# A four-layer graph network: the last batch's last tiles taken bank by bank, its output stored in three parts, the due times of layers 1 to 3 replaced

## The chip, the cores and the metric

The kernel runs on one core of a Trainium2 chip. A core has TensorE (PE; PEld is its weight load), VectorE (DVE), ScalarE (ACT), GpSimd (POOL) and SyncE (SP, which here issues most of the DMAs). The metric is the device time of one execution in microseconds (us). PSUM, where PE writes, has eight banks here, tiles `psc0` to `psc7`, each 128 x 512 f32.

## What is computed

There are 16 batches of 1024 nodes with 128 features, and an adjacency matrix for each. Every layer is x + gnn(relu(layernorm(x))). Layer 0 is a graph convolution with batch norms over all batches, so layers 1 to 3 can start only when all of it is done. Layer 1 and 3 are attention layers, layer 2 is one with scores from dot products. Cut to what matters:

```python
# layer 1 and layer 3 (layer 3 with an elu around it)
Wh = h @ W
e = leaky_relu((Wh @ a1)[:, :, None] + (Wh @ a2)[:, None, :])
out = softmax(where(adj > 0, e, -inf)) @ Wh
# layer 2
e = einsum('bid,bjd,dk->bkij', hidden, hidden, A)      # by the type of the edge, then leaky_relu
out = softmax(where(adj == 1, e[:, 0], ...)) @ hidden
```

## The kernel before, in words

**Tiles.** A batch is eight tiles of 128 nodes. The attention weights of one product are eight tiles `q[m]` of 128 x 1024 f32; they lie in ten rooms of SBUF (`xg6` to `xg15` in the profile's names) which all batches share. The product (`product`, L946) multiplies them with the values `v` of 128 x 129 (128 features and a column that sums the weights). Its output for the eight tiles of nodes lies in three PSUM banks, with three, three and two tiles (`TRI`). The weights of tile m give one step, here called a part: 8 matmuls that the profile counts as 16, L955, the banks in turn. So all three banks are complete only with the eighth part.

**A batch in layers 1 to 3** is the function `batch`. Layer 1 (`gat`, L989): norm, transpose (L932), scores and values (L996), the exponentials; the row of u is spread over all partitions, for the first batches by matmuls (L1034), for the others by a transpose (L1016), a copy (L1019), a send to DRAM (L1022) and a fetch from there (L1025). Then DVE weighs eight tiles (L1060), PE does eight parts, and `finish` takes reciprocals (L967), scales on ACT (L973) and adds (L985). Layer 2: norm with the power on POOL (L915) and the centring on DVE (L925), score matmuls in chunks of up to 512 columns (L1091), for each chunk two exponentials on ACT (L1099, L1095), larger and mask on DVE (L1109, L1112), transposes of the symmetric half (L1123) and their mask (L1127), eight parts, `finish`. Layer 3: `gat` again, then for each bank the reciprocal (L1141), two scalings for each tile of nodes on ACT (L1147), a join of two instructions on DVE (L1151, L1153). When all three banks are joined, one DMA of 512 KB stores the batch (L1161).

**Order.** Nothing is issued in the order in which it stands. Each piece of work is a step with an engine, an assumed duration, what it reads and writes and what rooms it needs. `Plan.attempt` places the steps one after another: for each engine it takes, among the steps that could begin within `WITHIN` of the earliest, the one with the lowest rank, and the rank is the due time of the step's batch less the longest assumed path from the step to the end. The result is a fixed order of instructions on each engine and a fixed room for each tile, PSUM banks included; the chip runs each engine's list in order, with waits between the engines. `DUES` has one due time for each batch, by its place in `order`: first the three batches whose adjacency is still in SBUF (13, 14, 15), then 0 to 12. A place is called a slot: slot 0 is batch 13, slot 15 is batch 12. At the same time some four batches are under way in different layers.

```python
rank = [due(s.group) - s.tail for s in self.steps]
...
order = sorted(kept["at"]) + [b for b in range(B) if b not in kept["at"]]
for b in order:
    batch(b)
plan.emit(lambda b: DUES[order.index(b)], WITHIN)
```

Of the kernel before, what the change touches and what calls it, by code (L numbers as in the profile page):

```python
# [19 lines left out]
P = 128  # L20

PAIRED = "(w p t) d -> p w t d"
# [11 lines left out]
LEVEL = 1638.0  # L34
XG_TILES = 6
WEIGHTS_AT = 40.0
L0_DUES, L0_WITHIN = [
    3.2, 51.2, 72.4, 90.5, 112.6, 124.5, 191.4, 204.9, 159.2, 265.6, 223.0, 273.4, 306.2, 325.8, 419.8, 408.3,
    419.5, 419.5,
], 0.1  # L40
DUES, WITHIN = [
    44.9, 60.2, 111.5, 81.6, 101.9, 124.9, 146.4, 167.9, 189.8, 211.1, 232.7, 254.2, 275.8, 297.5, 314.3,
    312.2,
], 0.02
GAT_LIMIT = 30.0
DOT_KEEP = 60.0
# [17 lines left out]
class Plan:  # L64
# [11 lines left out]
    def room(self, kind):  # L76
        return Room(kind)
# [10 lines left out]
    def step(self, engine, us, run, reads=(), writes=(), moved=0, group=0, also=(), since=0.0):  # L88
        s = Step(engine, us, run, moved, group, since)
        for k in reads:  # L90
            if k in self.writer:
                s.after.add(self.writer[k])
        for k in writes:
            if k in self.writer:
                s.after.add(self.writer[k])
            s.after.update(self.readers.get(k, ()))
        for k in reads:
            self.readers.setdefault(k, []).append(s)
        for k in writes:
            self.writer[k] = s  # L100
            self.readers[k] = []
        s.after.discard(s)
        for k in (*reads, *writes, *also):
            room = k[0] if isinstance(k, tuple) else k
            if isinstance(room, Room) and room not in s.rooms:
                s.rooms.append(room)
                room.uses += 1
        self.steps.append(s)
        return s
# [100 lines left out]
def groups_of(n, k):  # L210
    return [range(a, min(a + k, n)) for a in range(0, n, k)]
# [3 lines left out]
def gnn_stack(ctx: ExitStack, tc: tile.TileContext, x, adj, k1, b1, g1, be1, k2, b2, g2, be2,  # L215
# [52 lines left out]
    with tc.If(any_type == 0) as both:  # L268
        with tc.manual_schedule():
            plain_layers(tc, q_tiles, x, out, adj_t, gt_rows, u_rows, ident, ident_h, mhalf, gat1, gat3, edge, shift,  # L270
                         kcs, q9, rows9, held, kept)
# [5 lines left out]
def load_weights(nc, plan, rooms, tc, k1, b1, g1, be1, k2, b2, g2, be2, w1, a1, e0, w3, a3, edge, CB):  # L277
# [7 lines left out]
    def fetch(t, *parts):  # L285
        for n, (dst, src) in enumerate(parts):
            plan.step("sp", 0.1, lambda dst=dst, src=src: nc.sync.dma_start(dst(t), src), (),
                      [(id(t), n) if n else id(t)], 4096, 2, since=WEIGHTS_AT)

# [263 lines left out]
def norms(nc, plan, w, qall, q9, rows9, ident, ones, mhalf, gat1, gat3, edge, shift, kcs, flag, count):  # L553
# [93 lines left out]

    plan.step("dve", 0.8, choose, (), ["masks"], 0, 4, since=WEIGHTS_AT)
    group[0] = B + 1
# [141 lines left out]
def plain_layers(tc, q_tiles, x, out, adj_t, gt_rows, u_rows, ident, ident_h, mhalf, gat1, gat3, edge, shift,  # L791
                 kcs, q9, rows9, held, kept):
    nc = tc.nc
    B, N, D = x.shape
    NB = N // P
    WX = D + 3
    V1 = D + 1
    TRI = groups_of(NB, 3)
    ROW = [sum(NB - k for k in range(m)) * P for m in range(NB)]

    with ExitStack() as ctx:
# [28 lines left out]
            nc.gpsimd.memset(t, 0.0)  # L830
        for t in kinds["h1"]:
            nc.gpsimd.memset(t[:, :, D:V1], 1.0)
        plan = Plan(kinds)
        room = plan.room

        def batch(b):
            seat = room("seat")

            def step(engine, us_, run, reads=(), writes=(), moved=0, also=()):
                plan.step(engine, us_, run, reads, writes, moved, b, (seat, *also))  # L840
# [10 lines left out]
            at = plan.settled("at", kept["at"][b]) if b in kept["at"] else room("at")  # L851
# [94 lines left out]
            def ahead(m, acc):  # L946
                return acc if m > 2 else []

            def product(weights, done, values, V, acc):

                for m in range(NB):
                    def part(m=m):
                        for g, ns in enumerate(TRI):
                            for k, n in enumerate(ns):
                                nc.tensor.matmul(acc[g].ap[:, k * V1 : (k + 1) * V1],  # L955
                                                 weights[m].ap[:, n * P : (n + 1) * P], values.ap[:, m, :],
                                                 start=(m == 0 and k == 0), stop=(m == NB - 1),
                                                 skip_group_check=True)

                    step("pe", 1.88, part, [*done[m], *V], acc)  # L960
                return acc

            def over_sums(acc):
# [25 lines left out]
            def gat(layer, ext):  # L989
                y, gt, rs = norm(False)  # L990
                sc, ex, er, v, ub = (room(k) for k in ("tri", "tri", "col", "v", "ub"))
# [64 lines left out]
                q = [room("q") for _ in range(NB)]  # L1056
                acc = [room("ps") for _ in TRI]
                for m in range(NB):
# [2 lines left out]
                                                       ALU.max, ALU.mult)  # L1061

                    step("dve", 1.2, weigh, [(ub, 0), (ub, 4), ex, at], [q[m]], also=ahead(m, acc))
                return product(q, [[k] for k in q], v, [(v, "e"), *((v, ns[0]) for ns in TRI)], acc)

            finish(gat(1, gat1))

            y, ht, _ = norm(True)
# [10 lines left out]
            q = [room("q") for _ in range(NB)]  # L1079
            acc = [room("ps") for _ in TRI]  # L1080
            eu = room("eu")
            done = []
            for m in range(NB):
                e = room("e")
                wide = (NB - m) * P
                chunks = [range(c, min(c + 512, wide)) for c in range(0, wide, 512)]
                for c in chunks:
# [14 lines left out]
                    part = len(c) / 512  # L1102
# [28 lines left out]
                step("dve", 0.1 + 1.12 * wide / N, mask, [(eu, m), at], [(q[m], "u")], also=ahead(m, acc))  # L1131
                done.append([(q[m], "u"), *((q[m], ks[0]) for ks in groups_of(m, 4))])
            finish(product(q, done, h1, [h1], acc))

            acc = gat(3, gat3)
            rc, e3, r3 = room("col"), room("y"), room("y")
            for g, ns in enumerate(TRI):
# [19 lines left out]
                step("act", 0.52 * len(ns), scale, [acc[g], (rc, g)], [(e3, g), (r3, g)])  # L1157
                step("dve", 0.12 + 0.28 * len(ns), join, [(e3, g), (r3, g), *(X[n] for n in ns)], [(e3, g)])

            def store():  # L1160
                nc.sync.dma_start(out[b].rearrange(PAIRED, p=P, t=2), e3.ap.rearrange("p (w t) d -> p w t d", t=2))  # L1161

            step("sp", 0.06, store, [(e3, g) for g in range(3)], [("out", b)], P * N * 4)

        order = sorted(kept["at"]) + [b for b in range(B) if b not in kept["at"]]
        for b in order:
            batch(b)
        plan.emit(lambda b: DUES[order.index(b)], WITHIN)
# [493 lines left out]
```

## Time and profile before

| what | us |
|---|---|
| median of 3 runs (lowest, highest) | 1447.16 (1446.58, 1447.86) |
| the profiled execution | 1446.24 |
| its span in the profile | 1444.4 |
| PE busy, layers 1 to 3 well under way (600 to 800) | 197.34 of 200 |
| PE waiting, 420 to 1300, by the list of waits | ACT exponentials L1095 2.1 before L1091, masks L1127 2.0 before L1123 and 1.7 before L955 |
| granted clock 0.50 | from 368.1 to 378.3, between layer 0 and layer 1 |
| last matmul ends | 1433.1 |
| last join on DVE ends | 1438.5 |
| 512 KB stores, issue to landing | 2.9 to 3.8, median 3.0 |

How to read it: an engine's row in a timeline is start, duration, engine, line, operation, out<-in and the count of instructions in it; in square brackets stands the idle time just before, with the one who ended it. The list of stretches gives, for each engine, the time it was busy in a stretch. Matmuls overlap in their pipeline, so a busy PE can hide small waits; the distance between starts tells more, and that of L955's matmuls is 0.112 us.

### The profile page before, as it was taken

What the parts mean: (1) busy time and instruction counts of PE and PEld (TensorE: products, weight loads), DVE (VectorE), ACT (ScalarE), POOL (GpSimd) and SP (SyncE); (2) the same over time, 40 slices, a digit from 0 to 9 for tenths busy, and PEclk for the clock granted to TensorE, in tenths of its full rate; (3) what the DMA queues carried; (4) which work ended last, traced back from release to release, by engine and by line L of the source; (5) the groups of instructions that cost most, each with busy time, mean ns of one, the idle gap of its engine ahead of it and who ended that gap; (6) DMA issues with size and microseconds to landing.
All of it is one profiled execution on the core that took longest, in us unless ns stands there. A gap on an engine that the chain in (4) does not pass through costs nothing.

```text
span 1444.4 us, 30384 instructions
## 1 busy us (share of the span) xinstructions
PE 1389.4 (96%) x11710; PEld 1269.4 (88%) x11710; DVE 1105.2 (77%) x3154; ACT 794.6 (55%) x2123; POOL 366.1 (25%) x472
## 2 busy tenths in 40 slices
PE   4999999999999999999999999999999999999996
PEld 3889999898888999998989999898998898798896
DVE  4877665545778798897978878888889787797676
ACT  3766776765544763656464554636464744634652
POOL 7787677553310110110110101101111002010010
PEclk9999999999899999999999999999999999999998
DMA  9988988860300012111111212111111101010101
GB/s 157 150 179 163 142 144 148 140 66 2 117 1 16 31 45 88 60 45 59 45 60 45 74 39 91 61 47 60 45 59 45 45 30 45 16 44 16 45 31 47
DMA packets 56348, 99.05 MB, mean 69 GB/s; under 512 B 6297, under 2 KB 45569, under 8 KB 52865
## 3 DMA queue, kind: packets, MB, share of 16 engines
q1 hardware_dynamic: 37472, 79.17, 15.5%
q0 software_dynamic: 18720, 17.83, 14.3%
q8 instruction: 94, 1.54, 0.4%
q14 instruction: 62, 0.50, 0.1%
HBM read 118.37 MB, written 28.95 MB: 102 GB/s over the span
## 4 chain that ended last, share of the span: by engine, by line
PE 68%; DVE 18%; ACT 7%; DMA 3%; POOL 2%; issue 1%; DVEq 0%; POOLq 0%; ACTq 0%; SPq 0%
PE psc L955 31%; PE psa L498 7%; PE psa L458 7%; DVE xg L1060 6%; PE psc L1091 6%; PE gram L351 4%; PE psc L996 3%; PE psc L885 2%; PE psc L932 2%; DVE st L903 2%; ACT y L928 2%; PE psa L417 2%; PE psc L1123 2%; ACT eu L1099 2%; DVE y L925 2%; ACT e L1095 2%
## 5 line engine op out<-in xcount | busy, mean ns | idle before, releaser
L955 PE MATMUL psc<-v,xg 128*128 128x129 f32 x4096 | 483.1, 276 | 1.7 <-DVE xg L1060 1.3
L955 PEld LDWEIGHTS psc<-v,xg 128*128 128x128 f32 x4096 | 472.2, 192 | 14.2 <-issue 7.2
L955 PEld LDWEIGHTS psc<-h,xg 128*128 128x128 f32 x2048 | 239.4, 192 | 14.7 <-DVE xg L1127 6.5
L955 PE MATMUL psc<-h,xg 128*128 128x129 f32 x2048 | 249.7, 277 | 2.2 <-DVE xg L1127 1.7
L914 POOL TENSOR_SCALAR col<-mv 128x8 f32<-128x8 f32 x48 | 22.8, 475 | 896.1 <-DVE mv L909 722.0
L1060 DVE SCALAR_TENSOR_TENSOR xg<-ub,tri,at 128x1024 f32<-128x1024 f32 x176 | 217.5, 1276 | 9.4 <-DMA at<-adj_t 4.7
L1099 ACT ACTIVATE eu<-psc,shift 128x512 f32<-128x512 f32 x192 | 114.4, 596 | 162.8 <-PE psc L1091 150.1
L1091 PE MATMUL psc<-gt,gt 128*128 128x512 f32 (+3 forms) x384 | 152.7, 497 | 7.1 <-ACT e L1095 3.6
L425 ACT ACTIVATE at<-psa 128x1024 fp8e4<-128x1024 fp8e4 x128 | 131.3, 1033 | 42.1 <-PE psa L417 38.3
L1109 DVE SCALAR_TENSOR_TENSOR eu<-e,shift,eu 128x1024 f32<-128x1024 f32 (+7 forms) x128 | 103.8, 812 | 44.2 <-ACT e L1095 43.4
L458 PE MATMUL psa<-hv,a 128*128 128x257 f16 x1024 | 119.7, 276 | 4.3 <-DVE hv L400 3.3
L498 PE MATMUL psa<-rv,at 128*128 128x259 f16 x1024 | 119.6, 275 | 2.2 <-DVE g L505 2.0
L458 PEld LDWEIGHTS <-a 128*128 128x128 fp8e4 x1024 | 100.8, 99 | 19.6 <-issue 4.6
L498 PEld LDWEIGHTS <-at 128*128 128x128 fp8e4 x1024 | 99.6, 98 | 18.2 <-issue 2.7
L1095 ACT ACTIVATE e<-psc,shift 128x512 f32<-128x512 f32 x192 | 114.1, 594 | 0.0
L928 ACT ACTIVATE y<-xg,col 128x128 f32<-128x128 f32 x256 | 78.4, 394 | 56.9 <-DVE col L911 56.9
L973 ACT ACTIVATE y<-psc,col 128x128 f32<-128x128 f32 x256 | 71.2, 394 | 67.1 <-DVE col L967 47.7
L1147 ACT ACTIVATE y<-psc,col 128x128 f32<-128x128 f32 x256 | 69.1, 407 | 58.3 <-DVE col L1141 58.3
L1060 DVE SCALAR_TENSOR_TENSOR xg<-ub,tri,atc 128x1024 f32<-128x1024 f32 x80 | 98.9, 1276 | 0.8 <-DMA atc<-adj_t 0.8
L915 POOL TENSOR_TENSOR col<-col,mhalf 128x8 f32<-128x8 f32 x48 | 96.9, 2018 | 4.0
L470 POOL TENSOR_SCALAR rv<-r,cola 128x128 f16<-128x128 f32 x128 | 82.1, 651 | 59.5 <-DVE r L466 59.1
L1091 PEld LDWEIGHTS psc<-gt,gt 128*128 128x128 f32 x384 | 60.6, 191 | 32.0 <-issue 14.6
(214 smaller groups left out, 2004.0 us busy)
## 6 DMA issues: line engine op xcount, KB each, us to landing
a<-in_adj_dram POOLq DMA_DIRECT2D x128, 128.0 KB, 7.9
ub<-u_rows SPq DMA_DIRECT2D x29, 512.0 KB
xb<-in_x_dram SPq DMA_DIRECT2D x27, 512.0 KB, 5.6
adj_t<-at SPq DMA_DIRECT2D x13, 1024.0 KB, 4.3
at<-adj_t SPq DMA_DIRECT2D x8, 1024.0 KB, 4.8
out_dram<-y SPq DMA_DIRECT2D x16, 512.0 KB, 3.0
gt_rows<-xg SPq DMA_DIRECT2D x13, 512.0 KB, 8.4
xg<-gt_rows SPq DMA_DIRECT2D x13, 512.0 KB
```

The lines of the kernel that those rows point to most:

```text
L425: nc.scalar.activation(at.ap[:, i, :], ps.ap.bitcast(F8)[:, t::2], AF.Square, saturate=False, accum_out=sums.ap[:, i : i + 1])
L458: nc.tensor.matmul(ps.ap[:, : 2 * D + 1], block[:, i % 2 :: 2], hv.ap[:, j, :], start=(j == 0), stop=(j == NB - 1))
L470: nc.gpsimd.tensor_scalar_mul(rv.ap[:, i, 0:D], r.ap[:, i, :D], rc.ap[:, i : i + 1])
L498: nc.tensor.matmul(ps.ap[:, :W2], at.ap[:, i, j * P : (j + 1) * P], rv.ap[:, i, :], start=(i == 0), stop=(i == NB - 1))
L915: nc.gpsimd.tensor_tensor(rs.ap, va.ap, mhalf, ALU.pow)
L928: nc.scalar.activation(y.ap[:, n, :], xs(n), AF.Relu, bias=nm.ap[:, n : n + 1])
L955: nc.tensor.matmul(acc[g].ap[:, k * V1 : (k + 1) * V1], weights[m].ap[:, n * P : (n + 1) * P], values.ap[:, m, :], start=(m == 0 and k == ...
L1060: nc.vector.scalar_tensor_tensor(q[m].ap, ub.ap, ex.ap[:, m, 1:2], at.ap[:, m, :], ALU.max, ALU.mult)
L1091: nc.tensor.matmul(ps.ap[:, : len(c)], ha.ap[:, m * P : (m + 1) * P], ht.ap[:, m * P + c[0] : m * P + c[-1] + 1], start=True, stop=True)
L1095: nc.scalar.activation(e.ap[:, c[0] : c[-1] + 1], ps.ap[:, : len(c)], AF.Exp, bias=shift[:, 0:1], scale=1.0 - SLOPE)
L1099: nc.scalar.activation(eu.ap[:, ROW[m] + c[0] : ROW[m] + c[-1] + 1], ps.ap[:, : len(c)], AF.Exp, bias=shift[:, 1:2], scale=SLOPE)
L1109: nc.vector.scalar_tensor_tensor(t, e.ap[:, :wide], shift[:, 2:3], t, ALU.max, ALU.mult)
```

## The change

Three things. In layer 3 of the last batch in `order` (slot 15) the product does its first four tiles of weights as before; the last four become three steps, one for each bank, each with the four tiles' matmuls into that bank. The store of that batch becomes three DMAs: the first pair of node tiles (128 KB) when bank 0 is joined, two pairs (256 KB) when bank 1 is, the last pair (128 KB) when bank 2 is. And the sixteen due times are others, which gives all batches in layers 1 to 3 another order; layer 0 keeps its own.

```diff
+WHOLE = 4
 DUES, WITHIN = [
-    44.9, 60.2, 111.5, 81.6, 101.9, 124.9, 146.4, 167.9, 189.8, 211.1, 232.7, 254.2, 275.8, 297.5, 314.3,
-    312.2,
+    26.3, 47.2, 238.9, 112.2, 133.2, 154.3, 175.7, 197.2, 218.8, 240.4, 261.9, 283.6, 305.2, 326.7, 341.4,
+    341.6,
 ], 0.02
...
-            def product(weights, done, values, V, acc):
+            def product(weights, done, values, V, acc, whole=NB):
...
+                def part(ms, gs):
+                    for g in gs:
+                        for m in ms:
+                            for k, n in enumerate(TRI[g]):
                                 nc.tensor.matmul(acc[g].ap[:, k * V1 : (k + 1) * V1],
                                                  weights[m].ap[:, n * P : (n + 1) * P], values.ap[:, m, :],
                                                  start=(m == 0 and k == 0), stop=(m == NB - 1),
                                                  skip_group_check=True)
...
+                for m in range(whole):
+                    step("pe", 1.88, lambda m=m: part([m], range(len(TRI))), [*done[m], *V], acc)
+                left = range(whole, NB)
+                if left:
+                    for g, ns in enumerate(TRI):
+                        step("pe", 0.235 * len(ns) * len(left), lambda g=g: part(left, [g]),
+                             [*(d for m in left for d in done[m]), *V], [acc[g]])
...
-                return product(q, [[k] for k in q], v, [(v, "e"), *((v, ns[0]) for ns in TRI)], acc)
+                return product(q, [[k] for k in q], v, [(v, "e"), *((v, ns[0]) for ns in TRI)], acc,
+                               WHOLE if layer == 3 and b == order[-1] else NB)
...
+            if b != order[-1]:
+                step("sp", 0.06, lambda: store(slice(0, NB // 2)), [(e3, g) for g in range(len(TRI))], [("out", b)], P * N * 4)
+            else:
+                pairs = [min((ns[-1] + 1) // 2, NB // 2) for ns in TRI]
+                for g, n in enumerate(pairs):
+                    some = slice(pairs[g - 1] if g else 0, n)
+                    step("sp", 0.06, lambda some=some: store(some), [(e3, k) for k in range(g + 1)], [("out", b, g)], P * N * 4 * (some.stop - some.start) // (NB // 2))
```

By the instruction lists of the two built programs the lists of layer 0 are equal; from layer 1 on each engine's list has the same pieces of work in another order, except for the three bank steps and the two added stores. Slot 2's part of the work keeps its place late in the list (behind slot 12's), slots 14 and 15 change their parts in it: in the program before, slot 14 is the last to end, after the change slot 15.

More of the change, by code (lines that the diff above doesn't have):

```diff
@@ L832, in plain_layers @@
             nc.gpsimd.memset(t[:, :, D:V1], 1.0)
+        order = sorted(kept["at"]) + [b for b in range(B) if b not in kept["at"]]
         plan = Plan(kinds)
@@ L947, in ahead @@
                 return acc if m > 2 else []
-            def product(weights, done, values, V, acc):
[L951 to L954, printed above, removed]
+            def product(weights, done, values, V, acc, whole=NB):
[3 more added lines that the diff above has]
+                            for k, n in enumerate(TRI[g]):
                                 nc.tensor.matmul(acc[g].ap[:, k * V1 : (k + 1) * V1],
@@ L958, in part @@
                                                  skip_group_check=True)
-                    step("pe", 1.88, part, [*done[m], *V], acc)
+                for m in range(whole):
[5 more added lines that the diff above has]
+                             [*(d for m in left for d in done[m]), *V], [acc[g]])
                 return acc
@@ L1158, in batch, with store @@
                 step("dve", 0.12 + 0.28 * len(ns), join, [(e3, g), (r3, g), *(X[n] for n in ns)], [(e3, g)])
[L1160 to L1165, printed above, removed]
+            def store(some):
+                nc.sync.dma_start(out[b].rearrange(PAIRED, p=P, t=2)[:, some],
+                                  e3.ap.rearrange("p (w t) d -> p w t d", t=2)[:, some])
+            if b != order[-1]:
[5 more added lines that the diff above has]
+                    step("sp", 0.06, lambda some=some: store(some), [(e3, k) for k in range(g + 1)], [("out", b, g)], P * N * 4 * (some.stop - some.start) // (NB // 2))
         for b in order:
```

## The prediction

> **What bounds the kernel now.** I read the page's busy line first, then the stretches around the change, then the last 45 us engine by engine. A batch is called by its place in `order`: slot 0 to slot 15. Slot 15 is batch 12, the one the diff treats apart; slot 14 is batch 11. A "part" is the 16 L955 matmuls that use one tile of weights. The busy line, then stretches of the trace:
>
> ```profile
> PE 1389.4 (96%) x11710; PEld 1269.4 (88%) x11710; DVE 1105.2 (77%) x3154; ACT 794.6 (55%) x2123; POOL 366.1 (25%) x472
> ...
> ```
> ```profile
> 405.00:440.00 35.00, 32.64 (x254) 29.05 (x253) 24.24 (x58) 20.13 (x54) 5.31 (x3) 1.00 0.00 0
> 1389.00:1433.00 44.00, 43.79 (x391) 43.44 (x390) 30.96 (x64) 17.76 (x63) 3.00 (x2) 1.00 0.11 38
> 1433.00:1439.00 6.00, 0.08 (x1) 0.00 (x0) 4.06 (x12) 4.30 (x16) 0.00 (x0) 0.79 0.28 94
> 1439.00:1445.00 6.00, 0.00 (x0) 0.00 (x0) 0.00 (x0) 0.00 (x0) 0.00 (x0) 0.50 0.27 93
> ```
> The columns are PE, PEld, DVE, ACT and POOL busy, then the granted clock. PE is full until 1433 (43.79 of 44), and after it nothing is left but ACT, DVE and a store. So the time is PE's work, plus the holes in PE, plus the drain behind its last matmul. The change leaves PE's work alone: the same matmuls, each still loading its own weights. Only holes and drain can move.
>
> **The drain before.** DVE, ACT, then the SP queue:
> ```profile
> 1429.54 0.17 DVE L1141 RECIPROCAL col<-psc 128x2 f32<-128x2 f32 x1 [0.27 <-PE psc L955]
> ...
> 1433.94 0.16 DVE L1141 RECIPROCAL col<-psc 128x2 f32<-128x2 f32 x1
> 1435.03 0.56 DVE L1151 SCALAR_TENSOR_TENSOR y<-y,y 128x384 f32<-128x384 f32 x1 [0.93 <-ACT y L1147]
> ...
> 1437.64 0.42 DVE L1151 SCALAR_TENSOR_TENSOR y<-y,y 128x256 f32<-128x256 f32 x1
> 1438.10 0.42 DVE L1153 SCALAR_TENSOR_TENSOR y<-y,xg 128x256 f32<-128x256 f32 x1
> ```
> ```profile
> 1428.70 4.23 ACT L1147 ACTIVATE y<-psc,col 128x128 f32<-128x128 f32 x16 [19.67 <-DVE col L1141]
> 1433.27 4.30 ACT L1147 ACTIVATE y<-psc,col 128x128 f32<-128x128 f32 x16 [0.34 <-DVE col L1141]
> ```
> ```profile
> 1400.79 0.29 SPq L1022 DMA_DIRECT2D u_rows<-ur  x1
> 1402.02 0.32 SPq L1025 DMA_DIRECT2D ub<-u_rows  x1
> 1410.18 28.78 SPq L1161 DMA_DIRECT2D out_dram<-y  x3
> ```
> The last two batches end together, so ACT scales one (16 instructions, 0.265 apart) and then the other; DVE takes the reciprocals of their third banks at 1429.54 and 1433.94. PE's end is 1433.08 (T); the last join ends 1438.52 (T+5.4); the last store is issued 1438.6, lands about 3.0 later (median of the 512 KB stores), and the program ends at 1444.4 (T+11.3).
>
> **The drain after.** In the built program's instruction order PE now ends with slot 15 alone: slot 14's last part, then the last four weight tiles bank by bank. At 0.112 per matmul (16 in 1.79) those are 4 tiles x 6, 6 and 4 instructions = 24, 24 and 16: 2.69, 2.69, 1.79. So slot 14 is done at T-7.2, bank 0 at T-4.5, bank 1 at T-1.8, bank 2 at T. ACT: slot 14 from about T-7.9 (its first bank comes before its last) to T-3.7; bank 0 (6 x 0.265) to T-2.1; bank 1, released at T-1.4, to T+0.2; bank 2: its reciprocal at T+0.05, scale from T+0.35, four instructions to T+1.5. DVE's join of bank 1 (1.15) fits in T+0.35 to T+1.5, that of bank 2 (0.42 + 0.46) ends at T+2.45. That is 5.4 - 2.45 = **3.0 less**. The last store is a quarter, 128 KB. The nearest rows are the 4 KB send, 1.2 from issue to the next issue that waits for it (1400.79 to 1402.02), and the 512 KB store, 3.0: in proportion 1.65, so **1.3 less**; bounds 0 (no shorter) and 1.8 (like 4 KB). Two more issues cost SP 0.37 each, at T-0.3 and T+1.6, in front of nothing late. Drain: **-4.3**, bounds -3.0 and -4.8.
>
> The Trainium skill ("DMA: Bandwidth & Descriptors", Anatomy of one DMA) speaks against splitting: about 2.0 us per DMA is fixed, bytes / 436e3 come on top. That makes an estimate of 2.3 for the quarter, 3.2 for the whole, 0.9 saved; its fixed part is above the 1.2 that this trace shows for 4 KB.
>
> **PE holes in the last product.** Slot 14 now leads. From slot 14's u-row transpose (L1016, call it t) PE has 8.3 of work before its first part: three parts of slot 13 (5.4), slot 15's transposes and scores (2.7), one u-row. From such a transpose to the first weighing is 5.65 in the trace (1396.48 to 1402.13), so the fetch is hidden. But the instruction order shows two waits:
> - Slot 14's third bank is the bank that held slot 13's bank 0. It comes free when slot 13's first six scalings are over. DVE does two weighings (1.2 each), slot 15's row copy and scores before slot 13's reciprocals; chained with these rows, ACT finishes at t+10.8, PE wants the bank at t+9.7: **1.1**.
> - DVE then does, ahead of slot 15's first weighing: three weighings, the three joins of slot 13 (1.15, 1.15, 0.9) and columns. It ends at t+17.6; PE, four parts on, wants it at t+16.6: **1.0**. After this DVE (1.2 a tile) gains on PE (1.79).
> Before had one such wait, 0.4, at 1410.9 (weighing L1060 behind the joins). Difference **+1.7**, bounds 0 (DVE and ACT a little earlier) and +3.
>
> **PE holes at the start.** The order in layer 0 and up to slot 0's sixth part is unchanged. Then:
> ```profile
> 422.14 1.38 PE L932 MATMUL psc<-ident,y 128*128 128x128 f32 x8
> 424.39 3.84 PE L955 MATMUL psc<-v,xg 128*128 128x129 f32 x32 [0.86 <-DVE xg L1060]
> 428.06 1.88 PE L1091 MATMUL psc<-gt,gt 128*128 128x512 f32 x4
> 430.23 1.13 PE L1091 MATMUL psc<-gt,gt 128*128 128x512 f32 x2 [0.28 <-ACT v L1052]
> 431.19 1.05 PE L955 MATMUL psc<-v,xg 128*128 128x129 f32 x8
> ```
> Before, PE covers slot 0's way into layer 2 with parts of slot 1, and goes back to them between the score chunks (L1091). After, slot 0's eight parts run in one go (394.14 to 408.5), small steps follow (12.0 of work: mixes, transposes, the spread row), and slot 1's parts start only after seven score chunks. Slot 0's chain with the rows of before: to the aggregate 5.0, POOL 2.4, centre 2.1, transposes, relus, two weighings and the scaling 3.2, so scores at 421.25, a hole of 0.8. Each 512-wide chunk is 0.87 on PE and 1.15 on ACT (two exponentials, 0.57 each), and by the bank numbers six of the eight banks belong to slots 3 and 4, whose values stand behind the chunks on ACT. So PE follows ACT: chunks and values end at 430.4, the first part of slot 1 starts at 431.35; PE's work since 421.25 is 5.8, a hole of 4.3. Together 5.1, against 1.5 before (0.4 at 411.7, 1.1 at 423.2): **+3.6**. In return before's own later waits, 0.4, 1.0 and 1.2 at 429, 439 and 627, belong to an order that is gone; I take back 1.6 of these 2.6, since some will recur elsewhere. Net **+2.0**, bounds 0 and +3.6. From slot 6 on the order is the same period of 65 us, shifted, and slots 14 and 15 change roles: 0.
>
> **Sum.** +2.0 + 1.7 - 4.3 = -0.6 against 1446.24, the profiled execution (span 1444.4 and 1.8 around it): 1445.6. That execution lies 0.9 under the median of the runs, 1447.16; so a median of **1446.6**. About 0.2% (2.9 us) is what a measurement of this kernel can tell from no change.
>
> **Rivals.**
> 1. *The start's hole is filled* (chance 0.17): ACT takes the chunks earlier or the parts of slot 1 are not held back, and PE's place in the last product is kept half. 0 + 0.8 - 4.3 = -3.5: 1443.7. For it: ACT is busy only 20.13 of 35 us there. Against: the banks.
> 2. *The clock falls at the start* (0.10), slower. In 366 to 368.1 PE was busy half the time and no hole was over 1.6 us, yet the granted clock was 0.50 from 368.1 to 378.3:
> ```profile
> 364.70:368.10 3.40, 1.69 (x14) 1.36 (x13) 2.74 (x19) 1.07 (x2) 0.80 (x2) 1.00 0.00 0
> 422.70:426.10 3.40, 2.54 (x20) 2.11 (x19) 3.40 (x5) 2.03 (x3) 0.00 (x0) 1.00 0.00 0
> ```
> The stretch 426 to 429.5 would be about half busy after the change. Half clock for 10.2 us costs 5.1: -0.6 + 5.1 = +4.5, 1451.7. It decides from a PE share of about 0.5 (1.69 of 3.4 fell, 2.54 did not).
> 3. *The split saves only its work* (0.13): the quarter store lands as late as a whole one, and the start gives nothing back. +3.6 + 1.7 - 3.0 = +2.3: 1449.5, the change not doing in the drain what it is built to do.
> The forecast has 0.60, by itself 1444.3 to 1449.
>
> The Trainium skill ("TensorE: Matmul & The Clock Gate", Why this matters for your kernels) asks only that idle gaps stay under about 3 us. The trace has a fall with no gap above 1.6; by the rule rival 2 would be out.
>
> **Range and chances.** 1443.2 to 1450.2 holds rival 1 nearly whole, the forecast and rival 3's middle, and leaves out the clock. Faster by over 0.2%: 0.18 (rival 1 and 0.01); slower: 0.12 (rival 2 and a fringe of rival 3); within: 0.70.
>
> **What would show it.** Drain: from PE's last matmul to the last join 2.5 instead of 5.4, to the span's end 7.0 instead of 11.3, and three stores with the last landing 1.7 after its issue. Start: idle PE of 4 to 5 us between 418 and 432 with ACT (L1095, L1099) as releaser. End: idle PE ended by L1147 and L1060 in the last 40 us, some 2 us. The forecast is wrong if the start's hole is under 2, if the last product waits over 3, or if the clock row has a new 0.5.

## The result, and the profile after

Median 1453.39 us (1451.62 to 1456.77, 6 runs), the kernel before beside it 1447.51 (1445.57 to 1448.49, 6 runs): ratio 1.0040, 95% interval 1.0029 to 1.0051. The change costs some 5.9 us; 1446.6 with a range up to 1450.2 was predicted. The profiled execution is 1452.36, its span 1450.5 (1444.4 before).

After's page, busy line; then the start's 12 us in before; then in after the same 12 us, the stretches of the prediction and the drain (columns PE, PEld, DVE, ACT, POOL, then the granted clock):

```profile
PE 1390.2 (96%) x11710; PEld 1268.0 (87%) x11710; DVE 1108.2 (76%) x3154; ACT 794.0 (55%) x2123; POOL 361.0 (25%) x472
```
```profile
420.00:432.00 12.00, 10.85 (x75) 8.58 (x74) 8.05 (x18) 4.96 (x11) 0.97 (x1) 1.00 0.00 0
```
```profile
420.00:432.00 12.00, 8.41 (x29) 3.74 (x29) 11.06 (x33) 8.86 (x23) 1.90 (x2) 1.00 0.00 1
405.00:440.00 35.00, 31.38 (x234) 26.46 (x233) 29.35 (x83) 26.58 (x74) 5.71 (x6) 1.00 0.05 16
1389.00:1433.00 44.00, 41.28 (x365) 40.52 (x364) 34.49 (x68) 16.11 (x57) 2.51 (x3) 1.00 0.12 38
```
```profile
1389.00:1443.00 54.00, 50.92 (x449) 49.97 (x447) 39.58 (x83) 23.61 (x86) 2.51 (x3) 1.00 0.13 41
1443.00:1451.00 8.00, 0.00 (x0) 0.00 (x0) 1.82 (x4) 1.08 (x4) 0.00 (x0) 0.61 0.25 78
```

PE's work is the same (11710 matmuls, 0.8 us apart in sum), so nearly all of the 6 us is holes. At the start PE is short of 12 by 3.6 (by 1.15 before), and ACT and DVE have more to do than before; it is idle for 2.7 in the 44 us in which the kernel before had 0.21; and the tail without PE is shorter.

A busy PE hides small waits, so I measure the **lag**: I add up the matmuls that PE has begun, each with the usual distance between two starts of its shape, and see how much later than the kernel before a run reaches the same sum. The columns are the times of the kernel before; "drain" is from the start of the last matmul to the span's end; the last column is when and for how long the clock was granted at 0.50 ahead of the last matmul (without a time: it began between 366 and 372; before: 368.1, for 10.24).

| profile | 348 | 398 | 435 | 760 | 1380 | last matmul | drain | clock at 0.50 |
|---|---|---|---|---|---|---|---|---|
| before | 0 | 0 | 0 | 0 | 0 | 0 | 11.64 | 10.24 |
| after | 0.88 | 0.39 | 3.79 | 6.43 | 6.38 | 9.56 | 8.11 | 3.41 at 45, 3.41 at 376 |
| after once more (`after_again`) | -0.57 | -2.39 | 1.01 | 3.57 | 3.57 | 5.70 | 7.91 | 6.83 |
| its last store whole (`store_whole`) | -0.13 | -0.55 | 2.87 | 5.65 | 5.84 | 7.98 | 8.58 | 10.24 |
| its last tiles not by bank (`tiles_then_banks`) | 1.24 | 1.25 | 4.66 | 7.61 | 7.52 | 10.36 | 10.08 | 3.41 at 45, 10.24 |
| old code, slots 0 to 2 due as in the change (`start_alone`) | 0.20 | 0.16 | 3.56 | 5.44 | 5.77 | 6.23 | 11.57 | 10.24 |
| the change, old due times but for slots 14, 15 (`end_alone`) | 1.18 | 2.05 | 2.06 | 1.97 | 3.59 | 5.93 | 8.00 | 3.41 at 44, 10.24 |
| old order, last four tiles by bank (`frozen_end4`) | -0.10 | -0.22 | -0.21 | -0.24 | 0.35 | 1.27 | 8.02 | 10.24 |

Up to 398 the lists are equal, and what differs is the clock. After it, the lag grows by 3.40 between 398 and 435 in all five runs with the new start (by 3.1 if a matmul in progress is counted in proportion, and what follows grows by as much) and by 0.01 in the others. Where the start ends is a choice, for the lag is not smooth: 435 lies on a peak, ahead of a wait of 0.98 that only the kernel before has (at 439.85), so that after's lag is 2.25 at 440 and 1.99 at 450 before it climbs again. The sum of the start and what follows it does not depend on this choice. With the cut at 435 the parts of after's time are: 0.39 (clock), +3.40, +2.59 up to 1380 (nearly all before 760), +3.18 in the last product, -3.53 in the drain: +6.03.

**The start.** PE's timeline of after (start, duration, tile, and in brackets the idle time before and who ended it):

```profile
420.98 1.13 PE L1101 MATMUL psc<-gt,gt 128*128 128x512 f32 x2
423.47 1.98 PE L1101 MATMUL psc<-gt,gt 128*128 128x512 f32 x4 [1.36 <-ACT e L1105]
425.95 0.91 PE L1101 MATMUL psc<-gt,gt 128*128 128x384 f32 x2 [0.50 <-ACT e L1105]
...
428.04 1.56 PE L1101 MATMUL psc<-gt,gt 128*128 128x512 f32 x4 [0.66 <-ACT e L1105]
...
430.75 1.13 PE L1101 MATMUL psc<-gt,gt 128*128 128x512 f32 x2 [0.82 <-ACT e L1105]
431.71 3.51 PE L958 MATMUL psc<-v,xg 128*128 128x129 f32 x30
```

The score chunks (L1101) wait for ACT's exponentials (L1105) again and again, and the first part of slot 1 (L958) starts at 431.71; 431.35 was forecast, and 0.39 of the time is the clock's. **Behind the start**, from the same timeline, 452 to 660:

```profile
456.87 2.05 PE L958 MATMUL psc<-h,xg 128*128 128x129 f32 x16 [0.41 <-DVE xg L1137]
479.81 0.94 PE L1005 MATMUL psc<-gat,gt 128*128 128x131 f32 x6 [1.07 <-ACT gt L937]
...
544.21 14.56 PE L958 MATMUL psc<-v,xg 128*128 128x129 f32 x128 [1.13 <-DVE xg L1069]
582.77 0.66 PE L1133 MATMUL psc<-ident,eu 128*128 128x128 f32 x4 [0.69 <-DVE xg L1137]
```

No one place loses the 2.6: masks (L1137), relus (L937), weighings (L1069) are late here and there, until the period of the later slots is reached. Counted by the distance between starts, the waits over 0.2 between 435 and 760 are 14 in before, 7.1 us in sum, and 20 in after on the same work, 10.1 (10.0 to 10.1 in the other three profiles of the change in the table, 8.6 with the start alone).

**The last product** has the two waits that were forecast, 0.92 and 0.65, and a third that was not, 0.97 at slot 15's row transpose:

```profile
PE psc L1025 <- ACT tri L1018: 1.0, 1, 1.0
PE psc L958 <- ACT y L1157: 0.9, 1, 0.9
PE psc L958 <- DVE xg L1069: 0.6, 1, 0.6
PE psc L958 <- DVE ur L1028: 0.2, 1, 0.2
```

**The drain** on DVE in after: the reciprocals of the banks come from PE, bank 2's at 1442.67, and the last join ends at 1444.99, 2.63 behind the last matmul's start (5.72 before):

```profile
1440.89 0.18 DVE L1151 RECIPROCAL col<-psc 128x3 f32<-128x3 f32 x1 [0.67 <-PE psc L958]
...
1442.67 0.17 DVE L1151 RECIPROCAL col<-psc 128x2 f32<-128x2 f32 x1 [0.57 <-PE psc L958]
1442.85 0.56 DVE L1161 SCALAR_TENSOR_TENSOR y<-y,y 128x384 f32<-128x384 f32 x1
...
1444.11 0.43 DVE L1161 SCALAR_TENSOR_TENSOR y<-y,y 128x256 f32<-128x256 f32 x1
1444.57 0.42 DVE L1163 SCALAR_TENSOR_TENSOR y<-y,xg 128x256 f32<-128x256 f32 x1
```

### The profile page after: what moved, and what is told of

The parts are those of the page before. It is cut to its first block, busy times and chain, and to the rows that moved or that the text cites. A ratio compares the mean times of both kernels' runs of the same rounds, so it can differ in the third digit from the quotient of the medians.

```text
span 1450.5 us, 30394 instructions
## 1 busy us (share of the span) xinstructions
PE 1390.2 (96%) x11710; PEld 1268.0 (87%) x11710; DVE 1108.2 (76%) x3154; ACT 794.0 (55%) x2123; POOL 361.0 (25%) x472
## 4 chain that ended last, share of the span: by engine, by line
PE 66%; DVE 18%; ACT 7%; DMA 4%; issue 2%; POOL 2%; SPq 0%; DVEq 0%; POOLq 0%; ACTq 0%
PE psc L958 30%; PE psa L499 7%; PE psa L459 7%; DVE xg L1069 5%; PE psc L1101 5%; PE gram L352 4%; PE psc L1005 3%; PE psc L887 2%; DVE xg L1137 2%; ACT e L1105 2%; ACT eu L1109 2%; PE psc L934 2%; DVE st L905 2%; DVE y L927 2%; PE psa L418 2%
## 5 line engine op out<-in xcount | busy, mean ns | idle before, releaser
L958 PEld LDWEIGHTS psc<-v,xg 128*128 128x128 f32 x4096 | 472.5, 192 | 17.3 <-issue 9.7
L958 PE MATMUL psc<-v,xg 128*128 128x129 f32 x4096 | 483.8, 275 | 3.7 <-DVE xg L1069 2.6
L958 PE MATMUL psc<-h,xg 128*128 128x129 f32 x2048 | 249.8, 276 | 2.0 <-DVE xg L1137 1.4
L958 PEld LDWEIGHTS psc<-h,xg 128*128 128x128 f32 x2048 | 239.5, 192 | 13.7 <-DVE xg L1137 6.3
L916 POOL TENSOR_SCALAR col<-mv 128x8 f32<-128x8 f32 x48 | 19.0, 396 | 908.9 <-DVE mv L911 717.0
L1069 DVE SCALAR_TENSOR_TENSOR xg<-ub,tri,at 128x1024 f32<-128x1024 f32 x176 | 217.1, 1275 | 11.7 <-DMA ub<-u_rows 5.7
L1101 PE MATMUL psc<-gt,gt 128*128 128x512 f32 (+3 forms) x384 | 152.4, 496 | 9.7 <-ACT e L1105 6.9
L1105 ACT ACTIVATE e<-psc,shift 128x512 f32<-128x512 f32 x192 | 113.0, 589 | 0.0
L1069 DVE SCALAR_TENSOR_TENSOR xg<-ub,tri,atc 128x1024 f32<-128x1024 f32 x80 | 98.7, 1276 | 6.0 <-DMA atc<-adj_t 3.1
L1101 PEld LDWEIGHTS psc<-gt,gt 128*128 128x128 f32 x384 | 60.6, 191 | 35.4 <-issue 14.8
```

The costliest lines, as they stand in the source:

```text
L958: nc.tensor.matmul(acc[g].ap[:, k * V1 : (k + 1) * V1], weights[m].ap[:, n * P : (n + 1) * P], values.ap[:, m, :], start=(m == 0 and k == ...
L1069: nc.vector.scalar_tensor_tensor(q[m].ap, ub.ap, ex.ap[:, m, 1:2], at.ap[:, m, :], ALU.max, ALU.mult)
L1101: nc.tensor.matmul(ps.ap[:, : len(c)], ha.ap[:, m * P : (m + 1) * P], ht.ap[:, m * P + c[0] : m * P + c[-1] + 1], start=True, stop=True)
L1105: nc.scalar.activation(e.ap[:, c[0] : c[-1] + 1], ps.ap[:, : len(c)], AF.Exp, bias=shift[:, 0:1], scale=1.0 - SLOPE)
```

## The experiments

**Theory A**: the new order costs the time, in the start above all, and the bank steps and stores gain about what was forecast. **Theory B**: the bank steps or the split store cost it.

### The parts of the change alone

`dues_alone`: the old code with `DUES` of the change.

> The kernel before with the new due times alone: no bank steps, one store. Its lists of instructions are those of the changed kernel up to the last 40 us. Theory A (the new order costs the time, the split gains): PE lags before by 3.4 at 435 us and by 6.4 at 1300 us, as in the changed kernel; no shorter drain behind it; 1456 to 1460. Theory B (the bank steps and the three stores cost it): at most 2 us from before, 1446 to 1450.

Ratio 1.0059 [1.0045, 1.0073]: the due times alone cost as much as the whole change, or more. Lag 1.34 at 398, 4.73 at 435, 6.88 at 1380; drain 12.91.

`split_alone`: the old due times, bank steps and three stores on slot 14, which is the last to end there.

```diff
-                               WHOLE if layer == 3 and b == order[-1] else NB)
+                               WHOLE if layer == 3 and b == order[-2] else NB)
...
-            if b != order[-1]:
+            if b != order[-2]:
```

> The due times of before, the bank steps (last four tiles) and the three stores given to slot 14, which ends last under them. Lists as before up to the last 50 us, then other because the longest paths are other. Theory A: no lag until 1390; some new waits in the last product (1 to 5 us, since slot 14 is now put back behind slot 15), a drain of 7.9 instead of 11.3; 1446 to 1450. Theory B: 1452 or more.

1.0025 [1.0010, 1.0039], neither theory's. The lag is the same from 398 to 1380 (3.22, 3.11), then PE loses 6.01 and the drain saves 3.2: given bank steps, the planner arranges the last 50 us anew. A step that is cut in the source isn't the same step in the same place.

`stores_alone`: the same with `WHOLE = 8`, so that only the store is in three parts; the lists of PE, ACT and POOL are the old ones.

> The due times of before, whole parts, but slot 14 (last to end) stored in three parts. PE, ACT and POOL lists equal to before. The last join stays at 5.4 us behind PE; the quarter store saves 0.4 (as the changed kernel showed) to 1.3 (as predicted): 1446.2 to 1447.1. Theory B, if it is the stores that cost: over 1449.

0.9988 [0.9974, 1.0002]; no new hole in the last product (-0.11), drain 10.52: 1.1 shorter.

`frozen_end4`: the planned old order is kept; only slot 15's last two parts go ahead of slot 14's last four, these go by bank, the reciprocals, scalings and joins of both slots follow in that order, and slot 14 has the three stores. From the edit:

```diff
+    tail = mine[-BANKED:]
+    for n, s in zip(at, [order[n] for n in at if order[n] not in tail] + tail):
+        order[n] = s
...
+    for g in range(3):
+        tail[g].run = lambda g=g: part(ms, [g])
```

> The order of before kept instruction for instruction, but slot 15's last two parts go ahead of slot 14's last four, these four go bank by bank, and slot 14 is stored in three parts. Theory A: PE ends when it ended before (1433), the drain is 7.9 instead of 11.3: -3.5, 1444. Theory B: no gain, 1447 or more.

**0.9962 [0.9948, 0.9977], 1442.64 against 1448.36: faster than both kernels.** Holes in the last product 0.92, drain 8.02. Theory B falls: bank steps and stores gain 3.6 in the drain and cost 0.9 of holes when nothing else moves. That is 2.7 of the measured 5.7; the rest is not shown. Some of it may be the clock: over the span it was 0.995 to 0.996 in these four runs and 0.990 to 0.994 in the seven of the kernel before beside them, of which the shorter stretch at 0.50 behind PE's end (4.6 instead of 10.0 us) explains about half.

### Which due times

`start_alone`: the old code, with the change's due times of slots 0, 1 and 2 less the common shift of 29.3.

```diff
-    44.9, 60.2, 111.5, 81.6, 101.9,
+    -3.0, 17.9, 209.6, 81.6, 101.9,
...
```

> The kernel before, with the first three due times of the change (shifted by the 29.3 us by which all others are shifted): the start of the changed kernel, the end of before. If the start's order is what costs the 3.4 at 435 us: lag 3.4 to 4.3 there, and it is not given back: 4 to 6 at 1390, the last product and the drain as before, 1451 to 1454. If the later due times were needed for the loss: a lag under 2 at 1390.

1.0052 [1.0034, 1.0070]. +3.40 at the start, +2.2 behind it, 0.46 in the last product, drain 11.57: nearly the whole loss up to the last product (5.6 of 6.0), without any bank step. PE in the same 12 us of this run, and below of the old start (`end_alone`):

```profile
420.00:432.00 12.00, 8.42 (x29) 3.75 (x28) 11.06 (x34) 9.09 (x23) 1.90 (x2) 1.00 0.00 1
```
```profile
420.00:432.00 12.00, 11.14 (x83) 9.35 (x82) 9.55 (x20) 3.26 (x8) 2.94 (x2) 1.00 0.00 1
```

In the built program slots 0 and 1 alone give the same lists as all three, and slot 2 alone gives the old lists: it is the early slots 0 and 1.

`start_back`: the change with 74.2 and 89.5 for slots 0 and 1.

> The changed kernel with the due times of slots 0 and 1 put back (26.3 to 74.2, 47.2 to 89.5: the earlier ones plus the common shift of 29.3); the other fourteen, the bank steps and the three stores as in the change. In the built program PE's list is then the one of the kernel before up to its 7532nd row, some 50 us ahead of the end; the end is planned anew and has the bank steps last, with the third bank of the last batch released only behind the batch before. Theory A (the two early due times cost the time, 3.4 us by 435 us and some 2 more up to 700 us): the lag behind the kernel before, at equal work done on PE, stays within 0.5 us from the first layer's end to 1390 us; then the end of this list, between +1 and +6 us of holes as the other planned ends showed, less 3.5 of drain: a ratio of 0.998 to 1.002. Theory B (the bank steps and stores cost it): the lag is 0 too, and the ratio stays near the change's 1.004, with the drain no shorter than 11 us. A third: slot 2's late due time or the later slots' cost it, so that the lag is again 5 to 6 us by 760 us and the ratio 1.003 to 1.005.

1.0049 [1.0036, 1.0063], a miss, and its premise was wrong: in the traces PE's list leaves the old one at 438.6 us, not some 50 us ahead of the end. Slots 3 and 4 stand 1.3 and 2.0 later than before against the rest, and in the built program the old code with these two due times alone leaves the old lists of DVE and ACT at the same step (slot 2 alone moves nothing, as said). The start's hole is gone (0.93 at 398, 0.94 at 435), but the lag is 8.68 by 579 and 12.35 by 760. The time isn't a sum over due times; an undo counts only where the lists are shown to be equal.

`end_alone`: the change with the old due times plus 29.3 for slots 0 to 13.

```diff
-    26.3, 47.2, 238.9, 112.2, 133.2, 154.3, 175.7, 197.2, 218.8, 240.4, 261.9, 283.6, 305.2, 326.7, 341.4,
+    74.2, 89.5, 140.8, 110.9, 131.2, 154.2, 175.7, 197.2, 219.1, 240.4, 262.0, 283.5, 305.1, 326.8, 341.4,
```

> The changed kernel with the old due times plus the common shift of 29.3 for slots 0 to 13, and the change's for slots 14 and 15; bank steps and three stores as in the change. In the built program the lists of all engines are the old ones for about nine tenths of layers 1 to 3 (PE's list up to its row 6945 of 7532 there), then slots 14 and 15 change their parts. Theory A, with what the run with two due times put back taught (the order is not additive, so nothing but an equal list is a clean undo): the lag stays within 0.5 us, the clock's windows apart, as long as the lists are equal; the end makes 2 to 4 us of holes and saves 3.6 of drain: 0.998 to 1.001. Theory B (bank steps and stores cost the time): 1.003 to 1.005 with a lag of 0 up to there.

1.0002 [0.9993, 1.0011]. The lag stands still (2.05 at 398, 2.45 where the lists part), grows by 3.48 up to the last matmul, and the drain saves 3.64. So the change without its start is worth nothing, not a gain: what the end saves it pays for on PE.

`frozen_end3`: the kept order with three tiles by bank.

> The old order instruction for instruction, as in the run with the kept order and four tiles by bank (0.9962), but with only the last three tiles of slot 14 by bank: 18, 18 and 12 matmuls of 0.112 us instead of 24, 24 and 16. Theory A (the split gains whatever the order is kept from): 0.996 to 0.998. Bank 2 then takes 1.34 instead of 1.79 us, bank 1's six scalings of 1.6 us end later against PE's end (T+0.5 instead of T+0.2), and the last join at T+2.8 instead of T+2.6: 0.2 us slower than with four tiles in the drain, but 0.4 us fewer holes on PE if the weights' rooms come free earlier: the same within 0.1%. Theory B: 1.000 or slower.

0.9983 [0.9974, 0.9992]: faster than before again. Holes 0.39 instead of 0.92, but the last join 3.44 instead of 2.63 behind the last matmul's start (0.8 more where 0.2 was expected: DVE takes bank 2's reciprocal behind bank 0's joins, 1.0 behind the last matmul's start instead of 0.3) and a drain of 8.74. Its parts, 2.9 of drain less 0.4 of holes, come near the measured 2.7.

### The end

`scores_first`: the change, with two of slot 15's score steps (L1010) ahead of slot 14's first weighing on DVE.

> The changed kernel with two instructions of DVE moved: slot 15's second and third scores (L1010) go ahead of slot 14's first weighing, which waits for its fetched row. Theory: that waiting weighing holds the scores, these slot 15's exponentials, these PE's row transpose (1.1 and 0.3 lost on PE), and in turn slot 13's reciprocals and the bank wait (1.1). Without it PE loses 1.2 to 2.2 less in the last 45 us. Rival: the fetch itself is late and PE waits at the first part instead: no change.

1.0042 [1.0027, 1.0056]; holes in the last product 2.20 instead of 3.18. That looked like a hit, until other profiles with the unchanged order showed 2.13 and 1.70. The next run tells why.

`after_again`: the change itself once more.

> The changed kernel itself once more. In its first profile a 16 KB instruction fetch fell into the fetch of slot 14's spread row at 1407.3 us (7.5 us from the transpose to the first weighing, DVE 1.8 us idle), and into the last store at 1445.4 (1.7 us). If both are the chance of one execution, the fetch of the row takes 5.7 to 6.3 us here, the last product's holes come to 1.7 to 2.2 us as predicted instead of 3.2, and the span's end is 6.9 to 8 us behind the last matmul's start. If they belong to the program, as instruction fetches follow the instruction streams, the same 3.2 and 8.1 come back. The lag of 6.4 us at 1390 us comes back in both cases, less or more what the clock's half-speed windows in layer 0 and behind it make.

1.0041 [1.0027, 1.0054]. The profiled execution took 1448.2, its holes there 2.13. DVE in after and then in this run:

```profile
1407.52 0.17 DVE L1010 TENSOR_TENSOR tri<-psc,col 128x9 f32<-128x9 f32 x1 [4.94 <-PE psc L1005]
1409.51 1.28 DVE L1069 SCALAR_TENSOR_TENSOR xg<-ub,tri,at 128x1024 f32<-128x1024 f32 x1 [1.82 <-DMA ub<-u_rows]
1410.71 0.23 DVE L1010 TENSOR_TENSOR tri<-psc,col 128x9 f32<-128x9 f32 x2
```
```profile
1404.71 0.17 DVE L1010 TENSOR_TENSOR tri<-psc,col 128x9 f32<-128x9 f32 x1 [4.94 <-PE psc L1005]
1405.65 1.28 DVE L1069 SCALAR_TENSOR_TENSOR xg<-ub,tri,at 128x1024 f32<-128x1024 f32 x1 [0.77 <-DMA ub<-u_rows]
1406.85 0.23 DVE L1010 TENSOR_TENSOR tri<-psc,col 128x9 f32<-128x9 f32 x2
```

The weighing waits for slot 14's spread row (`ub`), and slot 15's scores stand behind it in DVE's list, so the fetch's delay goes through ACT's power (L1018) to PE. From the row's transpose to the weighing the five profiles with this order took 6.04, 6.47, 6.49, 7.18 and 7.52 us; their holes are 1.70, 2.13, 2.14, 2.84 and 3.18: each time the fetch less 4.34. `scores_first` had 6.70, so 2.36 by this rule and 2.20 measured: moving the scores is worth 0.16, the rest was the fetch. The queues of after while the fetch ran (1404.2 to 1409.1):

```profile
q1 hardware_dynamic: 144, 0.52, 35.8%
q8 instruction: 1, 0.02, 1.2%
q14 instruction: 1, 0.01, 0.8%
```

Beside the row's packets there is a 16 KB instruction fetch; 1.2% of 16 engines' 4.9 us is 0.93 us for this one packet. By the trace's packets it ran from 1407.33 to 1408.26, nearly all of the row was there by 1407.75, and its last packets came behind it, until 1409.06. The same late end is in `tiles_then_banks` and `start_back`: in these three the row took 4.5 to 4.8 from its issue to its last packet. In the five other profiles with this order, or nearly this order, the 16 KB fetch came earlier or when the row was all but in, and the row took 3.2 to 3.9.

`one_store`: the change, with one planned store at the end.

> The changed kernel with one 512 KB store at the end instead of three. If the size of the last store sets its landing: 1.1 to 1.3 longer drain. If the 16 KB fetch of instructions that begins 2.8 us after PE's end, and holds one DMA engine for 1.7 us, sets it: 0 to 0.5 longer.

1.0086 [1.0068, 1.0104]. It doesn't price the store: with another length of path behind them, the planner put slot 14's last part between the bank steps and bank 2's join behind all three of slot 14's, the last 6.53 behind the last matmul's start, drain 12.49.

`store_whole`: the change's lists, but the first two stores left out and the third whole.

```diff
-                    step("sp", 0.06, lambda some=some: store(some), [(e3, k) for k in range(g + 1)],
...
+                    step("sp", 0.06, lambda g=g: store(slice(0, NB // 2)) if g == len(TRI) - 1 else None,
+                         [(e3, k) for k in range(g + 1)],
...
```

> The changed kernel with its instruction lists on PE, DVE, ACT and POOL kept; on SP the first two of the three last stores are left out, and the third stores the whole 512 KB. It prices the quarter store by itself, which the run with one planned store could not, because the planner put the joins in another order there. The joins end 2.6 us behind the start of the last matmul as in the change. If a quarter store saves 1.3 us as predicted, the span's end is 9.4 us behind the last matmul's start instead of 8.1, in the case that no instruction fetch falls into the store; if the last landing is set by an instruction fetch of 1.0 to 1.7 us that falls into it, 8.1 to 9 us; the whole time is within 1.5 us of the change's either way, too little for a ratio.

1.0055 [1.0038, 1.0072]; drain 8.58. Issued at 2.71 behind the last matmul's start like the quarter, the whole store has its last packet 3.24 later; the quarter 3.37 and 2.91 later in the change's two profiles. The quarter saves 0.5 to 0.7 in the drain here, not 1.3; in `stores_alone`, where it was issued at 5.79, it saved 1.1, 0.6 up to its last packet and 0.5 behind it. The quarter's stretch in after (1445.0 to 1448.5, with the 256 KB store issued 1.0 ahead of it), then the whole store's in before (1438.5 to 1441.5):

```profile
q1 hardware_dynamic: 412, 0.39, 34.2%
q8 instruction: 1, 0.02, 3.0%
q14 instruction: 3, 0.02, 2.6%
```
```profile
q1 hardware_dynamic: 528, 0.52, 50.0%
q14 instruction: 3, 0.02, 2.5%
```

In after a 16 KB instruction fetch takes 3.0% of 16 x 3.5, 1.7 us, inside the store (it began at 1445.38, the store was issued at 1445.07). In before it began at 2.96 behind the last matmul, ahead of the store at 5.79. In all sixteen profiles this fetch comes 2.2 to 3.8 behind the last matmul's start, and quarter stores issued from 3.66 on take 2.1 to 2.2 (split and stores alone, and the two runs by tiles), the one at 3.52 takes 2.6, those at 2.71 take 2.8 to 3.4. The 256 KB store does not separate them, since it goes 0.8 ahead in the short ones and 1.0 in the long ones. That the fetch is the cause fits all of them; no run moved it. The prediction set the skill's estimates for the two sizes ("DMA: Bandwidth & Descriptors", Anatomy of one DMA: 2.3 and 3.2) against its own 1.65 and 3.0. That section gives the fit for DMAs that GpSimd issues, and these stores are SyncE's. The measured 2.1 to 2.2 for a quarter that no such fetch met is still nearer to the estimate of 2.3 than to 1.65, and the 0.5 to 0.7 saved to 0.9 than to 1.3; the 1.1 of `stores_alone` lies between.

`by_tile`: meant as the change with the last 64 matmul pairs in the order of tiles.

> The changed kernel with the last 64 matmuls in the order of the tiles again, all other instructions in their places: banks 0 and 1 complete 1.1 and 0.45 us before the end instead of 4.5 and 1.8. If the bank order makes the drain short: 2.7 us longer drain (10.8 instead of 8.1). If it is the order of slots 14 and 15 alone that does it: under 0.5.

1.0051 [1.0028, 1.0074], and no answer: the plan still took bank 0 as complete with its old step, so in this run bank 0's sums leave out the last tile of weights, and PE waited 0.91 for ACT to scale it. Done again as `tiles_then_banks`, with all 64 pairs ahead of the first reciprocal and the other engines' lists unchanged:

```diff
-                        step("pe", 0.235 * len(ns) * len(left), lambda g=g: part(left, [g]),
+                        step("pe", 0.235 * len(ns) * len(left),
+                             lambda g=g: [part([m], range(len(TRI))) for m in left] if g == 0 else None,
...
```

> The changed kernel with the last 64 matmul pairs on PE in the order of tiles instead of banks, all before the first bank is taken as complete; the lists of DVE, ACT, POOL and SP are equal to the change's, the three stores too. It does what the earlier run by tiles failed to do, whose first bank was scaled before the last tile's weights were in. All three banks are then complete at the last matmul only: sixteen scalings of 0.265 us (4.2) follow it instead of four, and the joins end 5.3 to 5.7 us behind the last matmul's start instead of 2.6; the span's end 10.8 to 11.2 behind it instead of 8.1. Theory A and the prediction's drain: 3.0 us slower than the change at the end alone, ratio to the kernel before 1.006. If the bank steps gained nothing (theory B), the drain stays at 8.1 to 9.

1.0063 [1.0047, 1.0078]; the last join 5.03 behind the last matmul's start instead of 2.63, the drain 10.08 instead of 8.11. The bank order is worth 2.4 of joins, 2.0 to 2.2 of drain.

## Why the prediction was wrong

- **Start, +3.6: right**, with the cut at 435. +3.40 in every run with the new start, 0.01 in those without; the releaser (the exponentials) and the place (the chunks ahead of slot 1's parts) are those named.
- **"In return before's own later waits ... belong to an order that is gone; I take back 1.6 of these 2.6": the step that failed.** On balance nothing came back: between 435 and 760 the new order lost 2.6 more (2.56, 2.78 and 2.95 in the other profiles of the change in the table, 1.9 with the start alone). The old waits did go: behind that at 439 the lag falls to 2.25, and behind that at 627 from 5.15 (at 625) to 3.44 (at 650). (That at 429 lies ahead of the cut and is in the +3.40.) But the prediction credited them and kept only 1.0 for waits that recur; the new order's own, of 0.4 to 1.1, were not looked for, and the waits of this stretch rose from 7.1 to 10.1. Net start +6.0 instead of +2.0: of the miss of some 6.5 us this is 4.
- From slot 6 on "the same period of 65 us, shifted": 0 held: 6.43 at 760, 6.38 at 1380. In between the lag goes up to 8.1 (at 925) and down to 6.0 (at 1125), and comes back.
- **Last product, +1.7: a size.** +3.18 in the first profile, 2.13 and 2.14 in others. The two waits are there (0.92 and 0.65 where 1.1 and 1.0 stood); the third came from the row's fetch, taken from one row as 5.65 and "hidden"; it took 6.0 to 7.5, and slot 15's scores were queued behind it. So the prediction's own sign, "if the last product waits over 3", came in the first profile and not in the second.
- **Drain, -4.3: a size.** The work's 3.0 was 3.09 (last join 5.72 to 2.63). The store's 1.3 was 0.4: its last packet came 0.58 later after its issue than before, and the program's end 1.03 earlier after that packet. Why the end follows a landing by 3.06 before and by 2.03 in after was not tried.
- **Rivals.** The first, a filled hole, did not come. The third had the nearest sum (+2.3): its store "as late as a whole one" is what happened, and it, too, took only the start's 3.6. The second, the clock: no 0.50 row at the start in any profile. The clock's windows as they lay in after; where it did fall in `start_back`, at 551.34; then a window of before behind which it did not fall, and one of `after_again` behind which it did:

```profile
420.72:424.13 3.41, 2.05 (x7) 0.82 (x7) 3.41 (x16) 1.49 (x4) 0.00 (x0) 1.00 0.00 0
424.13:427.54 3.41, 2.51 (x7) 0.64 (x5) 2.50 (x13) 2.91 (x6) 1.90 (x2) 1.00 0.01 2
427.54:430.96 3.42, 2.09 (x6) 1.03 (x7) 3.39 (x5) 3.42 (x11) 0.00 (x0) 1.00 0.00 0
```
```profile
547.93:551.34 3.41, 1.56 (x14) 1.27 (x13) 3.31 (x11) 0.64 (x4) 0.00 (x0) 1.00 0.00 0
551.34:554.75 3.41, 3.41 (x13) 2.81 (x13) 3.41 (x4) 3.00 (x10) 0.00 (x0) 0.50 0.97 288
```
```profile
40.39:43.80 3.41, 1.64 (x14) 1.13 (x12) 2.99 (x27) 3.27 (x8) 3.25 (x6) 1.00 1.07 84
```
```profile
363.00:366.41 3.41, 2.68 (x23) 2.30 (x21) 3.08 (x19) 0.79 (x2) 0.50 (x2) 1.00 0.00 0
```

PE's share was 0.60, 0.74 and 0.61 at the start of after, and 0.46 ahead of the fall at 551.34. That looks like the rival's point of about 0.5, but the point does not hold: the clock stayed behind a share of 0.48 and fell behind one of 0.79. What decides is open.

So most of the expected gain was there, 3.5 of drain, and went three ways, with more lost than gained: 3.4 to the start, 2.6 behind it, 2 to 3 to the last product. The order that the kernel had, with only its end rearranged, was faster in both its forms, by 0.4% and 0.2%; the traces' parts explain some 0.2%.

## What to carry to other kernels

A new order has to be priced over its whole way back to the steady period, not at the hole one can see; waits that an order loses are no credit before the new order's have been counted. When a planner orders the work, part and undo are clean only where the instruction lists are shown to be equal: writing out the old order and moving a few steps by hand gave what due times did not. A fetch or store that ends just in time should carry the spread of several executions, not one row's duration.

## What the runs showed of the hardware

- Instruction fetches run beside the kernel's data: single 16 KB packets of 0.92 to 1.82 us, in the last 50 us one every 3 to 22 us. In three profiles one fell late into the 512 KB fetch of a row, and the row's last packets came 1.3 to 1.4 behind the others (4.5 to 4.8 us from issue to last packet, 3.2 to 3.9 in five profiles without such a meeting). For the 128 KB store the times above fit the same reading; it was not tested.
- The granted clock falls for multiples of 3.41 us (3.41, 6.83, 10.24, 13.65 between layer 0 and 1), and where differs between executions of the same program: a fall at about 44 to 45 us is in seven of sixteen profiles, with a lag of 0.9 to 2.3 at 348 us (three of the seven have another at 24). It goes with the spread of the runs: of the 46 runs of the kernel before in the experiments, the 19 with a mean clock of 0.991 or 0.992 took 1448.5 on average, the four with 0.995 or 0.996 took 1445.9. The Trainium skill ("TensorE: Matmul & The Clock Gate", What's actually happening) has a window of 3413 ns that runs free of the kernel's start, which agrees with these lengths; its advice of gaps under about 3 us (Why this matters for your kernels) does not cover the fall at 551.34, ahead of which the longest wait was 1.85.
